# Two places of work in a four-layer graph network: row-wise endings in six later steps, and transposes held behind a maximum

## The chip, the cores and the metric

The kernel runs on one core of a Trainium2 chip. The metric is the device time of one execution in microseconds (us), the median of several runs. A core has five engines, each with its own instruction queue: PE (TensorE, matmuls), DVE (VectorE), ACT (ScalarE), POOL (GpSimd) and SP (SyncE, used here to issue DMAs). Engines wait for each other and for DMAs through semaphores.

## What is computed

A node matrix x of 4096 x 256 float32 goes through four attention layers over one adjacency matrix (4096 x 4096). Each layer adds its result to x and normalises the rows:

```python
# layer 0: additive attention, 4 heads          (the first layer)
x = _layernorm(x + _L0_gnn_ref(x, adj, L0_gnn_W, L0_gnn_a), axis=-1)
# layer 1: 4 heads of queries, keys and values  (the second layer)
x = _layernorm(x + _L1_gnn_ref(x, adj, L1_gnn_Wq, L1_gnn_bq, L1_gnn_Wk, L1_gnn_bk, L1_gnn_Wv, L1_gnn_bv), axis=-1)
# layer 2: additive attention, one head         (the third layer)
x = _layernorm(x + _L2_gnn_ref(x, adj, L2_gnn_W, L2_gnn_a), axis=-1)
# layer 3: cosine attention                     (the fourth layer)
x = _layernorm(x + _L3_gnn_ref(x, adj, L3_gnn_Wq, L3_gnn_Wk), axis=-1)
```

The two that matter here, cut to their core:

```python
def _L1_gnn_ref(x, edge, Wq, bq, Wk, bk, Wv, bv):
    q, k, v = (_split_heads(x @ W + b) for W, b in ((Wq, bq), (Wk, bk), (Wv, bv)))
    scores = jnp.einsum('hnd,hmd->hnm', q, k) / np.sqrt(HEAD_DIM)
    attn = jax.nn.softmax(scores + (edge.T - 1.0) * 10000.0, axis=-1)
    return jnp.einsum('hnm,hmd->hnd', attn, v)   # heads side by side again

def _L3_gnn_ref(features, adj, Wq, Wk):
    Qn = _cos_normalize(features @ Wq.T)
    Kn = _cos_normalize(features @ Wk.T)
    att = jax.nn.softmax(jnp.where(adj > 0, Kn @ Qn.T, NEG), axis=1)
    return 0.5 * (att @ features) + 0.5 * features   # every node has an edge to itself
```

## The kernel before

The 4096 rows are 32 tiles of 128 rows; four tiles make a block of 512 rows, so there are NB = 8 blocks of QB = 4 tiles. The rows x stay in SBUF as `X` for the whole kernel. The layers run one after the other, and each hands its last block's ending (`tail`) to the next, which weaves it into its own beginning.

How the order of instructions comes about: the program is unrolled and traced, and a planner then orders each engine's queue with a model of costs. Inside `tc.manual_schedule(engines=...)` the named engines keep the traced order. `tc.issue_after(ins)` keeps those instructions traced inside it that are on the engine of `ins` behind `ins` in that engine's queue. It adds no data dependence; the others go by the planner.

**The second layer's opening** (`multi_head_attention`, lines 727 to 825) makes keys, queries and values of all eight blocks before the attention starts. Only PE has its order written out there: `keys(0)`, the first layer's tail, `turn(1)`, and then for b from 1 to 7 `values(b - 1)` (16 matmuls of 256 columns) and `keys(b)` (32 matmuls of 512 columns; `values(6)` comes after `keys(7)`). `keys(b)` fills four PSUM banks one after the other; ACT copies each with its bias to `kT` or `qT` (L763), and DVE takes the greatest absolute value of each (`big`, L764), the queries' second half last. DVE adds the bias of the values and stores them in `V` (L781).

Every block of x is needed transposed (`xTs`). Blocks 0 and 1 are turned on PE. From block 2 on, `block_apart` (through `turning_apart`, L123 to L138) does it without PE: DVE transposes 32 x 32 squares in two halves into the tile `squares` (L129), one DMA writes them to DRAM as `far` (L133), and four DMAs read them back in their new place as `xT` (L137), all on SP's queue. `squares` has one buffer (`mh_sq`), so the next block's squares wait until the last block's write has landed. In the loop, block b + 1 is asked for in iteration b.

**The fourth layer** (`cosine_attention`) runs over blocks b of 512 queries and 32 tiles j of keys, as units (b, j). `scores` multiplies on PE (L1138), ACT takes the exponential (L1142). For two tiles at a time, a pair g = j // 2, `weights` multiplies by the mask on DVE (L1151) and `mix_weights` makes three more instructions (L443, L444, L445; the last is returned) for the seven-product scheme `product` (L453), which PE runs four units later (`LAG`). In the last block the last two pairs are without mix. The masks come from DRAM by POOL's DMA (L1070), 512 KB each, four buffers.

At the end of a block, `outputs` joins the products and `squares_far` turns them back: DVE transposes squares (L1172), SP writes four DMAs per half (`away`, L1176) and fetches the half back with one (`kept`, L1179). `outputs_far(b)` works on what was fetched (`back[b, 0]` and `back[b, 1]`): row sums (L1186), reciprocals, the rows themselves with their statistics (L1190, L156, L157), the inverse root (one DVE instruction, two of ACT, four of DVE), a scaling of each row (L186), and the store to `out` (L1203, SP). It is traced for block b - 1 when the products reach tile 10 of block b. This loop is not in a `manual_schedule`: the planner orders all engines. Only `ending`, for the last block, has its order written out.

```python
                for k in range(QB):
                    nc.vector.scalar_tensor_tensor(y[b][:, k, :], back[b, k // 2][:, k % 2, :], rden[:, k:k + 1], y[b][:, k, :],
                                                   OP.mult, OP.add)
                    one_row(mv, k, y[b][:, k, :])
                normalise([y[b][:, k, :] for k in range(QB)], mv)
                store(b, 0, QB, nc.sync)
```

Of the kernel before, what the change touches and what calls it, by code (L numbers as in the profile page):

```python
# [9 lines left out]
FP = mybir.dt.float32  # L10
# [8 lines left out]
P = 128  # L19
D = 256  # L20
# [8 lines left out]
def kernel(  # L29
# [121 lines left out]
    def block_apart(sb, once, dr, b, eng):  # L151
        return at_once(block_turning(sb, once, dr, X[:, b * QB:(b + 1) * QB, :], eng))

    def one_row(mv, k, y):
        st = fin.tile([P, 6], FP, name="bn")
        nc.vector.bn_stats(st, y)  # L156
        nc.vector.bn_aggr(mv[:, k, :], st)  # L157
# [553 lines left out]
    def multi_head_attention(w_sb, b_sb, tail, rows_of_den, rows_done, narrow_edges, ga):  # L711
# [12 lines left out]
        with ExitStack() as lay:  # L724
# [7 lines left out]
            with ExitStack() as pro:  # L732
                wp = pool(pro, "mh_w", 1)
                sb = pool(pro, "mh_in", 4)
                sq = pool(pro, "mh_sq", 1)
                own = pool(pro, "mh_o", 2)
                dr = pool(pro, "mh_far", 2, space=bass.MemoryType.DRAM)
                ps = pool(pro, "mh_ps", 6, space=PSUM)

                pv2 = pool(pro, "mh_pv", 2, space=PSUM)  # L740
                big = {n: wp.tile([P, NB, KC], FP, name=f"{n}big") for n in "qk"}
                xTs = {0: b_sb["x"]}

                def bank():
                    return ps.tile([P, QW], FP, name="g")

                def turn(b):
                    xTs[b] = transposed_block(sb, bank, b, (nc.scalar.copy, nc.scalar.copy))

                def keys(b):  # L750
                    for n, to, scale in (("k", kT, 1.0), ("q", qT, qscale)):
                        for o in range(KC):
                            pk = bank()
                            for c in range(KC):
                                nc.tensor.matmul(pk.rearrange("p (k i) -> p k i", k=QB),
                                                 w_sb[n][:, c, o * P:(o + 1) * P], xTs[b][:, c],
                                                 start=(c == 0), stop=(c == KC - 1))
                            part = to[:, o, b * QW:(b + 1) * QW]
                            if n == "q" and b > 1:

                                part, pk = (t.rearrange(how, a=QB, n=P // QB) for t, how in
                                            ((part, "p (k a n) -> p a k n"), (pk, "p (a k n) -> p a k n")))
                            nc.scalar.activation(part, pk, AF.Identity, bias=b_sb[n][:, o:o + 1], scale=scale)  # L763
                            nc.vector.tensor_reduce(big[n][:, b, o:o + 1], to[:, o, b * QW:(b + 1) * QW], AX.X, OP.max,  # L764
                                                    apply_absolute_value=True)

                def values(b):


                    for k in range(0, QB, KC):  # L770
                        pv = pv2.tile([P, KC, D], FP, name="pv")
                        for s in range(KC):
                            for c in range(KC):
                                nc.tensor.matmul(pv[:, s, :], xTs[b][:, c, k + s], w_sb["v"][:, c, :],
                                                 start=(c == 0), stop=(c == KC - 1))
                        for n in range(2):
                            j = slice(None, KC) if b > 1 else slice(None, 2 * KC - 1, 2)
                            first = 2 * b * QB + (n * QB + k if b > 1 else 2 * k + n)
                            j = slice(first, first + j.stop, j.step)
                            for r in range(2):  # L780
                                nc.vector.tensor_tensor(V[r * d:(r + 1) * d, j, :],  # L781
                                                        pv[n * d:(n + 1) * d, :, r * P:(r + 1) * P],
                                                        b_sb["v"][n * d:(n + 1) * d, r * P:(r + 1) * P].unsqueeze(1)
                                                        .to_broadcast([d, KC, P]), OP.add)

                def greatest():


                    top = {}
                    for n in "qk":  # L790
                        top[n] = wp.tile([P, KC], FP, name=f"{n}top")
                        nc.vector.tensor_reduce(top[n], big[n].rearrange("p b o -> p o b"), AX.X, OP.max)
                    nc.vector.tensor_tensor(top["q"], top["q"], top["k"], OP.mult)
                    most = wp.tile([P, KC * KC], FP, name="most")
                    for r in range(KC):
                        half = slice(r * d, (r + 1) * d)
                        pm = bank()
                        nc.tensor.matmul(pm[:, :KC], ones[half, :], top["q"][half, :], start=True, stop=True)
                        nc.vector.tensor_copy(most[:, r * KC:(r + 1) * KC], pm[:, :KC])
                    nc.vector.tensor_reduce(shift, most, AX.X, OP.max)  # L800
                    nc.vector.tensor_scalar(shift, shift, -1.0, ROOM, OP.mult, OP.add)
                    nc.vector.tensor_scalar_min(shift, shift, 0.0)

                with tc.manual_schedule(engines={mybir.EngineType.PE}):
                    keys(0)
                    tail(bank, own)
                    turn(1)
                    for b in range(1, NB):
                        if b < NB - 1:
                            xTs[b + 1] = block_apart(sb, sq, dr, b + 1, nc.sync)  # L810
                        if b < NB - 1:
                            values(b - 1)
                        keys(b)
                        if b == 2:
                            ga.spread(bank, w2_sb)
                    values(NB - 2)
                    greatest()
                    values(NB - 1)
# [293 lines left out]
    def cosine_attention(co, tail):  # L1112
# [4 lines left out]
        with ExitStack() as lay:  # L1117
# [8 lines left out]
            pa = pool(lay, "co_pa", 1, space=PSUM)  # L1126
            ps = pool(lay, "co_ps", 2, space=PSUM)
            ov = out.rearrange("(t p) d -> p t d", p=P)
            mixed, acc, prob, mix, y, back = {}, {}, {}, {}, {}, {}

            def bank():
                return ps.tile([P, QW], FP, name="g")
# [11 lines left out]
            def weights(b, g):  # L1144

                if b == 0 and g % 2 == 0:
                    t = mixed[g // 2] = keep.tile([P, 2, 4, P], FP, name=f"mixed{g // 2}")
                    mix_features(t, g // 2, nc.vector)
                    mix_sum(t, g // 2)
                z, lo = prob[b, g], 2 * g % MJ  # L1150
                nc.vector.tensor_tensor(z, z, co.mask[b, 2 * g // MJ][:, lo:lo + 2, :], OP.mult)  # L1151
                if b < NB - 1 or g < NP - LAST:
                    s = mix[b, g] = sb.tile([P, 4, HW], FP, name="mix")
                    mix_weights(s, z, nc.vector)

            def one_product(b, g, n):
                product(acc[b], prob[b, g], mix[b, g], mixed[g // 2][:, g % 2], g, n)
# [21 lines left out]
                nc.sync.dma_start(t, away.rearrange("r a m q s -> a r (m q s)"))  # L1179
                back[b, h] = t.rearrange("p (k f) -> p k f", k=2)  # L1180

            def outputs_far(b):
                mv = fin.tile([P, QB, 2], FP, name="mv")
                rden = fin.tile([P, QB], FP, name="rden4")
                for h in range(2):
                    nc.vector.tensor_reduce(rden[:, 2 * h:2 * h + 2], back[b, h], AX.X, OP.add)  # L1186
                nc.vector.tensor_scalar_mul(rden, rden, 2.0 / D)
                nc.vector.reciprocal(rden, rden)
                for k in range(QB):
                    nc.vector.scalar_tensor_tensor(y[b][:, k, :], back[b, k // 2][:, k % 2, :], rden[:, k:k + 1], y[b][:, k, :],  # L1190
                                                   OP.mult, OP.add)
                    one_row(mv, k, y[b][:, k, :])
                normalise([y[b][:, k, :] for k in range(QB)], mv)
                store(b, 0, QB, nc.sync)

            def rest(b, k, po, rden, mv):
                nc.vector.scalar_tensor_tensor(y[b][:, k, :], po, rden, y[b][:, k, :], OP.mult, OP.add)
# [88 lines left out]
                store(b, 3, 1, nc.sync)  # L1286

            units = [(b, j) for b in range(NB) for j in range(NT)]
            LAG = 4
            steps = {(0, j + n): (NB - 2 + b, step) for b, j in enumerate((1, 12)) for n, step in ((0, 3), (4, 3), (5, 1), (7, 2), (8, 3))}  # L1290
            for i in range(len(units) + LAG):
                if i < len(units):
                    b, j = units[i]
                    seen = scores(b, j)
                    if j % 2:
                        weights(b, j // 2)
                    if (b, j) == (0, 3):
                        tail(bank, cp)
                    if (b, j) == (0, 0):
# [4 lines left out]
                if i >= LAG:  # L1304
# [7 lines left out]
                    if i - LAG < len(units) - 2 * LAST:  # L1312
                        for n in range(7)[:4] if j % 2 == 0 else range(7)[4:]:
                            one_product(b, j // 2, n)
                        if j == NT - 1:
                            outputs(b)
                    if b and j == 10:
                        outputs_far(b - 1)
            with tc.manual_schedule(engines={mybir.EngineType.PE, mybir.EngineType.DVE, mybir.EngineType.Activation}):
                ending(NB - 1)  # L1320

# [89 lines left out]
```

## Time and profile before

| | |
|---|---|
| runs | 2788.82, 2796.16 and 2797.37 us, median 2796.16 us |
| profiled execution | 2794.14 us, its span 2792.4 us |
| PE busy | 2772.5 us, 99% of the span |
| DVE busy | 2290.4 us, 82% |
| ACT busy | 1702.9 us, 61% |
| POOL busy | 1082.3 us, 39% |
| second layer's opening | 723 to 813 us of the span |
| fourth layer | 2160 us to the end |

Times in a trace are counted from the start of the span. A profile names an instruction by the line of the program, so L129 or L186 may be that of a helper which several layers use; the tile's name and the time tell them apart. In the lists of waits the columns are: who waited for whom, total us, times, the longest. In the timeline they are: start, duration, engine, line, operation, written and read tiles with their shapes, how many; in square brackets stands how long the engine had been idle before, and what ended that. In the chain of waits they are start, duration and the piece of work.

### The profile page before, as it was taken

How to read it: one execution, taken by the hardware profiler on the slowest of the kernel's cores; microseconds unless marked ns; L12 is line 12 of the kernel's file. 1: busy time of each engine (PE TensorE's matmuls, PEld its weight loads, DVE VectorE, ACT ScalarE, POOL GpSimd, SP SyncE). 2: the span in 40 equal slices, each digit the busy share in tenths (PEclk: the TensorE clock that was granted, in tenths of full speed). 3: DMA queues.
4: the chain of work that ended last, by engine and by line, in shares of the span. 5: the costliest groups of instructions: out<-in, count | busy, mean ns of one | idle time of the engine just before them, and what ended most of it. 6: DMA issues, size and time to landing. Idle time of an engine off the chain costs nothing. (4 is left out here: it accounts for less than half of the span.)

```text
span 2792.4 us, 50485 instructions
## 1 busy us (share of the span) xinstructions
PE 2772.5 (99%) x19557; PEld 1449.7 (52%) x19557; DVE 2290.4 (82%) x3049; ACT 1702.9 (61%) x2668; POOL 1082.3 (39%) x1020
## 2 busy tenths in 40 slices
PE   9999999999999999999999999999999999999999
PEld 5333333333453333333333335888888777776776
DVE  8899999999677788887888878888888877776776
ACT  8899999999336666666666666465556422222222
POOL 0000100100029878778788787455455000000000
PEclk9999999999999999999999999999999999999999
DMA  7566676765339899998988988567778554444442
GB/s 207 107 142 137 138 144 130 136 143 114 69 97 193 184 178 196 192 188 184 195 182 189 190 182 187 174 199 213 181 207 238 109 82 76 77 72 78 72 74 43
DMA packets 275066, 411.94 MB, mean 148 GB/s; under 512 B 54809, under 2 KB 155657, under 8 KB 273930
## 3 DMA queue, kind: packets, MB, share of 16 engines
q0 software_dynamic: 104176, 182.74, 41.4%
q1 hardware_dynamic: 164280, 218.88, 26.2%
q10 hardware_dynamic: 6370, 7.10, 0.8%
q8 instruction: 153, 2.51, 0.4%
q14 instruction: 87, 0.71, 0.1%
HBM read 335.94 MB, written 39.40 MB: 134 GB/s over the span
## 5 line engine op out<-in xcount | busy, mean ns | idle before, releaser
L854 DVE TENSOR_TENSOR prob<-p,mask 128x1024 f32<-128x1024 f32 x512 | 619.7, 1222 | 165.9 <-ACT p L844 159.6
L844 ACT ACTIVATE p<-p,shift 128x1024 f32<-128x1024 f32 x512 | 555.7, 1088 | 319.4 <-PE p L842 319.2
L312 PE MATMUL acc<-prob,V 128*32 128x512 f32 x6144 | 664.0, 592 | 1.2 <-DVE prob L302 1.2
L299 ACT ACTIVATE prob<-row,dst 128x512 f32<-128x512 f32 x1020 | 635.1, 714 | 0.6
L302 DVE SCALAR_TENSOR_TENSOR prob<-prob,mask 128x2048 f32<-128x2048 f32 x256 | 580.4, 2286 | 25.7 <-ACT prob L299 25.0
L864 POOL TENSOR_TENSOR den<-den,prob 128x1024 f32<-128x1024 f32 x220 | 558.5, 2539 | 92.5 <-DVE prob L854 87.2
L842 PE MATMUL p<-qT,kT 64*64 64x512 f32 x4096 | 531.1, 590 | 2.2 <-DVE prob L854 2.2
L878 PE MATMUL acc<-prob,V 64*64 64x512 f32 x4096 | 529.9, 589 | 0.0
L312 PEld LDWEIGHTS acc<-prob,V 128*32 128x32 f32 x6144 | 197.3, 110 | 453.0 <-issue 432.2
L453 PE MATMUL acc<-mix,mixed 128*128 128x256 f32 x1476 | 402.1, 381 | 4.8 <-DVE mix L444 2.9
L453 PEld LDWEIGHTS acc<-mix,mixed 128*128 128x128 f32 x1476 | 278.7, 190 | 49.4 <-DVE mix L444 4.1
L878 PEld LDWEIGHTS acc<-prob,V 64*64 64x64 f32 x4096 | 157.4, 133 | 282.1 <-issue 280.3
L842 PEld LDWEIGHTS p<-qT,kT 64*64 64x64 f32 x4096 | 154.3, 133 | 279.2 <-issue 254.5
L90 POOL COPY tick<-prob 128x1 f32<-128x1 f32 x35 | 38.0, 1086 | 642.8 <-DVE prob L302 641.9
L1151 DVE TENSOR_TENSOR prob<-prob,mask 128x1024 f32<-128x1024 f32 x128 | 156.1, 1219 | 141.6 <-ACT prob L1142 141.6
L870 POOL DMA_DIRECT2D den<-prob x240 | 230.9, 962 | 61.2 <-DMA den<-prob 24.6
L1070 POOL DMA_DIRECT2D mask<-in_adjT x64 | 47.7, 745 | 532.6 <-DVE prob L1151 436.9
L453 PE MATMUL acc<-prob,X 128*128 128x256 f32 x984 | 252.6, 379 | 0.0
L453 PEld LDWEIGHTS acc<-prob,X 128*128 128x128 f32 x984 | 186.7, 190 | 78.8 <-issue 57.1
L586 DVE SCALAR_TENSOR_TENSOR prob<-r,own,mask 128x512 f32<-128x512 f32 x252 | 177.0, 743 | 49.0 <-POOL mix L445 13.0
L1142 ACT ACTIVATE prob<-p 128x512 f32<-128x512 f32 x144 | 86.0, 597 | 202.8 <-PE p L1138 202.8
L1142 ACT ACTIVATE prob<-g 128x512 f32<-128x512 f32 x112 | 66.9, 597 | 208.4 <-PE g L1138 208.4
(239 smaller groups left out, 2849.5 us busy)
## 6 DMA issues: line engine op xcount, KB each, us to landing
mask<-in_adjT SPq DMA_DIRECT2D x254, 512.0 KB
den<-prob POOLq DMA_DIRECT2D x240, 512.0 KB, 5.3
mask<-edges SPq DMA_DIRECT2D x512, 64.0 KB
mask<-in_adjT POOLq DMA_DIRECT2D x64, 512.0 KB, 5.7
edges<-in_adj POOLq DMA_DIRECT2D x32, 512.0 KB, 9.7
far<-squares SPq DMA_DIRECT2D x16, 512.0 KB
den<-prob SPq DMA_DIRECT2D x16, 512.0 KB
row<-far SPq DMA_DIRECT2D x7, 1024.0 KB
```

What stands on the lines that cost most here:

```text
L299: nc.scalar.activation(z[:, h, :], r, AF.Relu, bias=-1.0, scale=dst[:, j, h:h + 1])
L302: nc.vector.scalar_tensor_tensor(z, z, 1.0, mask[m][:, j % MJ, :].unsqueeze(1).to_broadcast([P, H, QW]), OP.add, OP.mult)
L312: nc.tensor.matmul(acc[b][h * G:(h + 1) * G, n, :], part, prob[b, j][:, h, :], start=(j == 0), stop=(j == NT - 1))
L453: nc.tensor.matmul(acc[at][:, half * HW:(half + 1) * HW], w, a, start=(g == 0 and n in (0, 2, 3, 5)), stop=(g == NP - 1), skip_group_check ...
L586: nc.vector.scalar_tensor_tensor(z[:, n, :], r, ga.own[:, j:j + 1], mask[:, n, :], OP.add, OP.mult)
L842: nc.tensor.matmul(p[c * d:(c + 1) * d, r, :], kT[half, c, at:at + d], qT[half, c, cols], start=True, stop=True)
L844: nc.scalar.activation(p, p, AF.Exp, bias=shift)
L854: nc.vector.tensor_tensor(z, p, mask[m][:, j % MJ, :].unsqueeze(1).to_broadcast([P, KC, QW]), OP.mult)
L864: nc.gpsimd.tensor_tensor(to, to, flat, OP.add)
L870: nc.gpsimd.dma_start(to, flat, accum_op=OP.add)
L878: nc.tensor.matmul(acc[b][c][r * d:(r + 1) * d, :], V[half, j, r * d:(r + 1) * d], prob[b, j][half, r, :], start=(j == 0), stop=(j == NH - 1))
L1151: nc.vector.tensor_tensor(z, z, co.mask[b, 2 * g // MJ][:, lo:lo + 2, :], OP.mult)
```

## The change

In the fourth layer `outputs_far(b)` is cut into six steps. `weights` now returns the last mix instruction, and the loop keeps it as `mixes`. Steps 0 to 5 for block b - 1 are traced when the products have reached tiles 15, 17, 19, 21, 23 and 25 of block b, after the scores and weights of the unit four further on; each is inside `issue_after(mixes)`, so that its DVE instructions stay behind that mix. Step 0 makes the sums and reciprocals, steps 1 and 2 two rows each, step 3 begins the root, step 4 ends it and scales two rows, step 5 scales two and stores.

In the second layer `keys` returns its last maximum, and `block_apart(b + 1)` is traced inside `issue_after` of the maximum that `keys(b - 1)` returned. The first call of the loop (block 2) has none; block 3 is held behind block 1's, and so on to block 7 behind block 5's. Only the DVE squares are held by it, as the DMAs are issued from SP.

```diff
                             nc.scalar.activation(part, pk, AF.Identity, bias=b_sb[n][:, o:o + 1], scale=scale)
-                            nc.vector.tensor_reduce(big[n][:, b, o:o + 1], to[:, o, b * QW:(b + 1) * QW], AX.X, OP.max,
-                                                    apply_absolute_value=True)
+                            last = nc.vector.tensor_reduce(big[n][:, b, o:o + 1], to[:, o, b * QW:(b + 1) * QW], AX.X,
+                                                           OP.max, apply_absolute_value=True)
+                    return last
...
                     turn(1)
+                    last = None
                     for b in range(1, NB):
                         if b < NB - 1:
-                            xTs[b + 1] = block_apart(sb, sq, dr, b + 1, nc.sync)
+                            with tc.issue_after(getattr(last, "ins", last)) if last is not None else nullcontext():
+                                xTs[b + 1] = block_apart(sb, sq, dr, b + 1, nc.sync)
                         if b < NB - 1:
                             values(b - 1)
-                        keys(b)
+                        last = keys(b)
...
                 if b < NB - 1 or g < NP - LAST:
                     s = mix[b, g] = sb.tile([P, 4, HW], FP, name="mix")
-                    mix_weights(s, z, nc.vector)
+                    return mix_weights(s, z, nc.vector)
...
-            def outputs_far(b):
...
+            def outputs_far(b, step, seen):
+
+                with tc.issue_after(getattr(seen, "ins", seen)):
+                    if step == 0:
+                        rden = fin.tile([P, QB], FP, name="rden4")
+                        for h in range(2):
+                            nc.vector.tensor_reduce(rden[:, 2 * h:2 * h + 2], back[b, h], AX.X, OP.add)
+                        nc.vector.tensor_scalar_mul(rden, rden, 2.0 / D)
+                        nc.vector.reciprocal(rden, rden)
+                        norm[b] = rden, fin.tile([P, QB, 2], FP, name="mv")
+                    elif step < 3:
+                        rden, mv = norm[b]
+                        for k in (2 * step - 2, 2 * step - 1):
+                            nc.vector.scalar_tensor_tensor(y[b][:, k, :], back[b, k // 2][:, k % 2, :], rden[:, k:k + 1],
+                                                           y[b][:, k, :], OP.mult, OP.add)
+                            one_row(mv, k, y[b][:, k, :])
+                    elif step == 3:
+                        norm[b] += begin_root(norm[b][1])
+                    else:
+                        _, mv, v, r, n = norm[b]
+                        if step == 4:
+                            end_root(v, r, n)
+                        for k in (2 * step - 8, 2 * step - 7):
+                            scale_row(y[b][:, k, :], mv, r, k)
+                        if step == 5:
+                            store(b, 0, QB, nc.sync)
...
-            LAG = 4
+            LAG, mixes = 4, None
...
                     if j % 2:
-                        weights(b, j // 2)
+                        mixes = weights(b, j // 2) or mixes
...
-                    if b and j == 10:
-                        outputs_far(b - 1)
+                    if b and j in (15, 17, 19, 21, 23, 25):
+                        outputs_far(b - 1, (j - 15) // 2, mixes)
```

More of the change, by code (lines that the diff above doesn't have):

```diff
@@ L1128, in cosine_attention @@
             ov = out.rearrange("(t p) d -> p t d", p=P)
-            mixed, acc, prob, mix, y, back = {}, {}, {}, {}, {}, {}
+            mixed, acc, prob, mix, y, back, norm = {}, {}, {}, {}, {}, {}, {}
             def bank():
@@ L1180, in squares_far @@
                 back[b, h] = t.rearrange("p (k f) -> p k f", k=2)
-            def outputs_far(b):
[L1183 to L1194, printed above, removed]
+            def outputs_far(b, step, seen):
[23 more added lines that the diff above has]
+                            store(b, 0, QB, nc.sync)
             def rest(b, k, po, rden, mv):
```

## Prediction

> **What bounds the kernel now.** I read the page first. TensorE (PE) is busy 99% of 2792.4 us; its clock is full in nearly all slices. So only time in which PE stands still, or runs slowly after a pause, can be won. Next, PE's waits by stretch. In the fourth layer (2160 to 2793 us) there is one wait of PE itself, and one group of VectorE (DVE) waits that could be behind it:
>
> ```profile
> DVE rden L1186 <- DMA kept<-away: 16.8, 8, 6.9
> ...
> PE acc L453 <- DVE mix L444: 2.9, 1, 2.9
> ```
>
> [...]L1186 is the first instruction of `outputs_far`: it reads the rows fetched back from DRAM. The timeline shows how one wait becomes the other:
>
> ```profile
> 2573.62 0.74 POOL L1070 DMA_DIRECT2D mask<-in_adjT  x1 [8.73 <-DVE prob L1151]
> ...
> 2573.64 0.56 SPq L1179 DMA_DIRECT2D kept<-away  x1
> ...
> 2581.00 0.69 DVE L1186 TENSOR_REDUCE rden<-kept 128x2 f32<-128x512 f32 x1 [6.95 <-DMA kept<-away]
> 2581.60 0.42 DVE L444 TENSOR_TENSOR mix<-prob,mix 128x256 f32<-128x256 f32 x1
> ...
> 2582.07 1.27 PE L453 MATMUL acc<-mix,mixed 128*128 128x256 f32 x4 [2.88 <-DVE mix L444]
> ...
> 2583.14 1.91 PE L1138 MATMUL g<-T,T 128*128 128x512 f32 x2
> ```
>
> The fetch is issued in the same moment as a 512 KB mask load and takes 7.4 us. The planner has put L1186 between L443 and L444, so two instructions of the running pair of tiles stand behind it. PE then waits 2.88 us and runs slowly (1.91 us for a score that takes 1.02 elsewhere). The chain of waits has the same place:
>
> ```profile
> 2557.72 5.54 DMA away<-kept
> 2564.59 8.97 DMA away<-kept
> 2573.64 7.34 DMA kept<-away
> ```
>
> What does it cost? The first `away` issues of the seven blocks start at 2251.52, 2327.99, 2403.91, 2479.82, 2555.73, 2636.48 and 2712.39: distances 76.47, 75.91, 75.92, 75.91, 80.75, 75.91. The undisturbed block is 75.91 us, so the fifth event costs 4.84 us, the first (DVE waited 4.05 us) 0.56, the others nothing though DVE waited up to 1.78. Together 5.40 us.
>
> The second layer's opening (723 to 813 us) has three DVE waits for the squares buffer, 11.3 us, the longest 6.1:
>
> ```profile
> 733.02 1.30 DVE L129 STREAM_TRANSPOSE squares<-X 128x512 f32<-128x512 f32 x2 [6.09 <-DMA far<-squares]
> 734.25 0.64 DVE L764 TENSOR_REDUCE kbig<-kT 128x1 f32<-128x512 f32 x1
> ...
> 736.86 0.42 ACT L230 ACTIVATE neg<-neg 128x256 f32<-128x256 f32 x1 [5.16 <-DVE neg L229]
> ...
> 737.18 1.05 ACT L119 COPY xT<-g 128x512 f32<-128x512 f32 x2
> ...
> 737.80 3.70 PE L755 MATMUL g<-xT,wk_sb 128*128 128x512 f32 x8 [1.19 <-ACT xT L119]
> ```
>
> Read upwards: PE waits for ScalarE's (ACT) copies of block 1, these stand behind a `neg` that waits for DVE, and DVE stands still with block 3's squares, as the single buffer still holds block 2's. Everything behind is late too. Undisturbed, `keys` takes 6.87 us and `values` 3.44 (760.77 to 767.64, 767.64 to 771.09). Here `keys(1)` starts at 737.80 rather than 736.44 (1.36), lasts 7.27 (0.40), and `values(1)` lasts 4.08 (0.64): 2.40 us lost.
>
> **The Trainium skill.** "Perfetto Trace Analysis", Tensor Engine Instruction, says that ACT and DVE are strict FIFO: a blocked instruction blocks all behind it. Both pictures agree. "DMA: Bandwidth & Descriptors", Queues, rings and completion order, says that each engine shares itself in turn among the queues with work, so a mask load slows a fetch beside it; the trace agrees in that fetch (7.4 us, against 5.5 at 2268.42). "TensorE: Matmul & The Clock Gate", Part 1, says that an idle stretch halves the array's clock for a while; the 1.91 us after the pause, against 1.02, fits.
>
> **The change, part by part. (a) Fourth layer.** Instructions, bytes and engines stay the same; `outputs_far` becomes six steps, each held behind the last mix instruction (L445) of the running pair. Step 0 is traced after unit (b, 19), pair 9; the fetch starts after pair 1. A pair takes 4.74 us: eight pairs are 37.9 us, so step 0 starts about 38 us after the first `away` issue. The latest landing seen is 25.3 us after it (2581.0 - 2555.7), so 13 us remain and DVE should not wait. What stands behind each step on DVE is the next pair's mask product. DVE's pair is 1.22 + 0.69 + 0.42 + 0.42 = 2.75 us and then about 1.87 idle (L1151 waits for ACT). Step 0: 2 x 0.683 + 0.164 + 0.172 = 1.70. Steps 1 and 2: 2 x (0.467 + 0.418 + 0.174) = 2.12 each. Step 3: 0.17 plus two ACT instructions of 0.2. Step 4: 4 x 0.16 and two scalings of 0.35, 1.3. Step 5: 0.7. Only steps 1 and 2 exceed the idle, by 0.25 us each. PE reads a pair's mix about 4.06 us after it is ready (2769.54 against 2773.60), so 0.5 us is hidden; without that cover it would cost 0.5 us a block, 3.5 in all. Step 3's exponentials stand in ACT's queue before later `prob`; in the third event, ACT waited 1.71 us for this and PE lost nothing.
>
> The store (SP) moves to about 61 us after the first `away`, before the next at 75.9: nothing of SP's is behind it then. For the last block it is issued near 2770 rather than 2742.69, while the final stores start at 2787.68; 512 KB should be gone by then. Step 5 is behind pair 13's mix at 2769.54, where DVE is free until 2771.41: free. Buffers: the fetched rows are needed until step 2, at pair 11, and overwritten after the next block's end; `y` has two buffers and its next user comes later than the store. Sum of (a): -5.40 us.
>
> **(b) Second layer.** Block 3's squares now stand behind the last queries' maximum of block 1 (750.53), and so on. The 6.09 us wait at 727 goes: DVE does the maxima and the row tail about 4 us earlier, `neg` and the copies are ready near 734.5, before PE needs them at 736.4. That returns the 1.36 us and most of the 1.04 behind it. Bounds: 0 to 2.40, I take 2.0. The price is lateness. From the end of block 7's squares (780.14) its turned rows are landed by 786.5: 6.4 us through two DMAs in SP's queue. After `keys(5)` ends (788.28) the maximum ends at 789.89, two halves of squares take 1.30 and the trip 6.4: 797.6, against `keys(7)` at 798.60, which has no `values` before it. 1.0 us remain. Blocks 3 to 6 have 3.44 us more. DVE's values sums (L781) come 1.3 us later, and PE takes that buffer again only 17 us later. Before SP's next issues (817.76) the queue is empty. Sum of (b): -2.0.
>
> **Sum.** Profiled execution 2794.14 - 5.4 - 2.0 = 2786.7 us. The runs shown are 2788.82, 2796.16 and 2797.37. 2794.14 - 5.40 = 2788.74 is almost the lowest: I read the scatter as more or fewer such fetch waits, an inference. So I do not add the 2.0 us by which the median lies above the profiled execution; against the median it is -9.5 us, or -0.34%. About 0.3% (8.4 us) is what a measurement can tell from no change.
>
> **Rivals. B: the opening returns nothing.** The order on DVE is the planner's there, and another instruction may hold the copies, or the 1.0 us of block 7 is used up. For: the whole tail of the first layer sits on DVE there. Against: DVE stands idle 6 us just before. 2794.14 - 5.4 = 2788.7.
>
> **C: the steps press on the pairs.** DVE's idle is smaller than steps 1 and 2, and ACT may wait at step 3 as at 2281.55 (3.95 us, where that pair of PE took 0.30 longer). At 0.3 to 0.6 us a block over seven: 2.1 to 4.2 back, hence 2789 to 2791. Against: in four events all of this work within two or three pairs cost nothing.
>
> **D: slower, the turn becomes the second layer's bound.** If the planner puts the eight L781 (3.5 us) ahead of the squares and the write takes 7.5 us, as block 2's did (725.53 to 733.02), rather than 2.7, the maximum's 1.6, 3.5, 1.3 and the trip of 11.2 make 17.6 against the 13.75 from the end of `keys(b-1)` to the start of `keys(b+1)`: 3.9 us late at block 3, again at block 5, and 7.3 at block 7, where only 10.3 lie between: 15.1 in all, so 2794.14 - 5.4 + 15.1 = 2803.8. It costs from a trip of 7.3 us behind those sums, and outweighs the fourth layer's gain from 8.0. Against: the mask loads that slowed that write are over by then (DMA is idle from 744 on).
>
> The change not doing what it says: were the planner's order unchanged by the edges, the time would be 2794; but the squares before 750 us and L1186 before pair 9 are ruled out by them.
>
> **How the numbers follow.** Forecast A 0.62, B 0.18, C 0.12, D 0.08. A spans 2784.5 to 2788; with B and C the range is 2784.5 to 2791, leaving out D and a little. Faster by over 0.3% (below 2787.8): most of A and a little of B, 0.58; within 0.3%: 0.34; slower: 0.08.
>
> **What would show it.** Right: no DVE wait for `kept<-away`; `away` distances of 75.9 in all blocks; no PE wait in front of `keys(1)`; squares of block 3 after the maximum of block 1. Wrong: PE waiting in front of `keys(7)` or `keys(3)`, ACT waiting over 4 us for step 3's variances (L182), or a run-to-run scatter as wide as before, which would mean that it came from elsewhere.

## The result and the profile after

| | before | after |
|---|---|---|
| median | 2790.87 us (2788.21 to 2797.37, 14 runs) | 2786.06 us (2785.25 to 2788.96, 14 runs) |
| profiled execution | 2794.14 us, span 2792.4 | 2785.99 us, span 2784.2 |
| PE busy | 2772.5 us | 2768.9 us |

The ratio after to before is 0.9982, 95% interval [0.9975, 0.9988]: about 5 us less. The forecast of 2786.7 us lies 0.6 us above the median of the changed kernel. The gain is smaller than forecast: 0.18% rather than 0.34%, since before's median over 14 runs is 2790.87 us and not the 2796.16 of the three runs that I had. The interval lies clear of 1, so the prediction's 0.3% as the least that can be told from no change was too coarse.

In the program after the change `outputs_far`'s sums are L1191 (L1186 before), the mask product L1154 (L1151), the away writes L1179 and the fetch L1182 (L1176, L1179), the mask load L1073 (L1070). The first view is the timeline of the fifth block after, with the same moment as the one shown of before:

```profile
2568.89 0.56 SPq L1182 DMA_DIRECT2D kept<-away  x1
2570.28 0.74 POOL L1073 DMA_DIRECT2D mask<-in_adjT  x1 [8.73 <-DVE prob L1154]
...
2590.16 0.43 DVE L445 TENSOR_TENSOR mix<-prob,mix 128x256 f32<-128x256 f32 x1
2590.50 1.27 DVE L1191 TENSOR_REDUCE rden<-kept 128x2 f32<-128x512 f32 x2
...
2595.24 0.87 DVE L1198 SCALAR_TENSOR_TENSOR y<-kept,rden,y 128x256 f32<-128x256 f32 x2
...
2596.69 0.30 DVE L157 BATCH_NORM_AGGREGATE mv<-bn 128x2 f32<-128x6 f32 x2
2597.19 1.23 DVE L1154 TENSOR_TENSOR prob<-prob,mask 128x1024 f32<-128x1024 f32 x1 [0.20 <-ACT prob L1145]
```

The sums come straight behind L445, with no bracket: DVE did not wait. They start 38.1 us after the block's first `away` issue (2552.38); the fetch had been issued 21.6 us earlier. After step 1 DVE is still idle for 0.20 us before the next mask product, waiting for ACT, so the step fits. In the list of waits of this layer the two rows shown of before (`rden` for `kept<-away`, `acc` for `mix`) no longer occur. The seven first `away` issues start at 2248.73, 2324.64, 2400.55, 2476.46, 2552.38, 2628.29 and 2704.20: six distances of 75.91 or 75.92.

The second view is the timeline of the second layer's opening after:

```profile
732.63 0.42 ACT L230 ACTIVATE neg<-neg 128x256 f32<-128x256 f32 x1 [1.11 <-DVE neg L229]
...
732.96 1.05 ACT L119 COPY xT<-g 128x512 f32<-128x512 f32 x2
...
736.27 3.60 PE L755 MATMUL g<-xT,wk_sb 128*128 128x512 f32 x8
...
746.31 0.67 DVE L764 TENSOR_REDUCE qbig<-qT 128x1 f32<-128x512 f32 x1
...
746.91 1.29 DVE L129 STREAM_TRANSPOSE squares<-X 128x512 f32<-128x512 f32 x2
```

ACT's copies of block 1 end at about 734.0, over 2 us before PE needs them, and `keys(1)` starts with no wait. Block 3's squares stand behind the last maximum of block 1, as the edge says. DVE's three waits for the squares buffer (11.3 us before) are gone.

To see where a difference lies I cut each execution at four instants: the start of `keys(0)`, the first attention score of the second layer, the first and the last of the fourth layer's first `away` issues. "Opening" is between the first two, "middle" between the second and third, "blocks lose" is the sum of six distances less 6 x 75.91. The end after the last issue is 80.0 us in all of them. The experiments are told below. Each row is one profiled execution, in us, and experiments ran on different chips:

| execution | opening | middle | blocks lose | its time |
|---|---|---|---|---|
| before | 89.59 | 1438.49 | 5.40 | 2794.14 |
| before, second profile (e12_plain) | 89.79 | 1441.93 | 4.85 | 2797.22 |
| before, third profile (e13_plain) | 89.71 | 1440.67 | 1.77 | 2793.85 |
| after | 87.22 | 1438.25 | 0 | 2785.99 |
| after again (e9_both) | 87.21 | 1438.65 | 0 | 2786.61 |
| opening alone (e1_opening) | 87.21 | 1438.61 | 0.68 | 2786.88 |
| opening alone again (e10_opening) | 87.21 | 1440.58 | 1.95 | 2790.95 |
| fourth layer alone (e2_fourth) | 89.25 | 1438.48 | 0 | 2787.53 |
| fourth layer alone again (e11_fourth) | 89.41 | 1437.30 | 0 | 2787.56 |
| late, in one piece (e4_onepiece) | 89.77 | 1439.87 | 0 | 2790.20 |
| six steps, early (e5_early) | 89.50 | 1440.26 | 9.8 | 2799.41 |
| two squares buffers (e3_twobuf) | 91.87 | 1441.42 | 6.5 | 2800.45 |
| only block 3 held (e8_block3) | 87.21 | 1443.96 | 1.7 | 2793.56 |
| one block back (e6_oneback) | 133.92 | 1443.96 | 1.0 | 2839.41 |

From before to after, profile against profile, the span falls by 8.2 us: 2.37 in the opening, 5.40 in the blocks, 0.24 in the middle, 0.18 ahead of `keys(0)`.

### The profile page after: what moved, and what is told of

It reads as the page before. It is cut to its first block, busy times and chain, and to the rows that moved or that the text cites. A ratio compares the mean times of both kernels' runs of the same rounds, so it can differ in the third digit from the quotient of the medians.

```text
span 2784.2 us, 50486 instructions
## 1 busy us (share of the span) xinstructions
PE 2768.9 (99%) x19557; PEld 1449.1 (52%) x19557; DVE 2299.5 (83%) x3049; ACT 1703.4 (61%) x2668; POOL 1080.8 (39%) x1020
## 5 line engine op out<-in xcount | busy, mean ns | idle before, releaser
L1154 DVE TENSOR_TENSOR prob<-prob,mask 128x1024 f32<-128x1024 f32 x128 | 156.3, 1221 | 142.9 <-ACT prob L1145 142.9
L1073 POOL DMA_DIRECT2D mask<-in_adjT x64 | 47.6, 743 | 526.9 <-DVE prob L1154 508.3
```

## The experiments

The first four shared one chip and the kernel before on it (median 2791.68 us, 2787.37 to 2797.84, 56 runs). Those runs form two heaps, 38 from 2787.4 to 2792.7 and 18 from 2794.0 to 2797.8.

**The opening alone.** The kernel before with the second layer's part of the change only.

```diff
-                            xTs[b + 1] = block_apart(sb, sq, dr, b + 1, nc.sync)
+                            with tc.issue_after(getattr(last, "ins", last)) if last is not None else nullcontext():
+                                xTs[b + 1] = block_apart(sb, sq, dr, b + 1, nc.sync)
...
-                        keys(b)
+                        last = keys(b)
```

> The second layer's part alone, the fourth layer as before. My theory: the opening falls from 89.6 us (723.4 to 813.0) to 87.2 us as in the kernel after, without a PE wait in front of keys(1), and the fourth layer keeps its waits for the fetched rows, some 10 to 20 us of DVE waits in total and blocks of 75.9 us plus now and then 0.5 to 5 us. Time: 2.4 us below before, in every run alike; the runs stay scattered over 5 us or more. Rival (the scatter comes from the opening, where a far write lies beside loads): the scatter shrinks to about 2 us here and the time falls by 4 us or more.

Measured: 2787.79 us (2786.03 to 2788.73, 12 runs), ratio 0.9985 [0.9976, 0.9993]. In the profile the opening takes 87.21 us, the whole 2.4 less. The fourth layer still waits for its fetches, as its list of waits says (total, times, longest):

```profile
DVE rden L1189 <- DMA kept<-away: 10.4, 6, 4.0
...
PE acc L453 <- DVE mix L444: 0.2, 1, 0.2
```

The longest wait here is 4.0 us where before had 6.9, though this layer's instructions stand in the same order on every engine: the same program part can lose 0.68 us in one execution and 5.40 in another. The gain by the median (3.9 us) is more than the opening's 2.4 and the scatter of 2.7 us less than I expected: both figures are nearer to the rival's than to mine. The interval holds 2.4 and 3.9 alike. The repetition below comes back to it.

**The fourth layer alone.** The six late steps, the opening as before.

```diff
-                    if b and j == 10:
-                        outputs_far(b - 1)
+                    if b and j in (15, 17, 19, 21, 23, 25):
+                        outputs_far(b - 1, (j - 15) // 2, mixes)
```

> The fourth layer's part alone, the second layer as before. My theory: no DVE wait for the fetched rows, all seven distances of the first away issues at 75.9 us, opening still 89.6 us; median 2 to 3 us below that of before (5.4 below a run with waits such as the profiled one), and the runs within about 2 to 3 us of each other. Rival (scatter from the opening): scatter as wide as before.

Measured: 2788.46 us (2786.32 to 2792.11, 21 runs), ratio 0.9984 [0.9978, 0.9991]. All six distances are 75.91 or 75.92 and DVE does not wait for `kept<-away`. But the runs still scatter over 5.8 us: what goes up and down from run to run is not the fetch waits alone.

**Late, but in one piece.** Are the steps needed, or only the later place? `outputs_far` is left whole and traced at tile 15, behind the mix of pair 9.

```diff
-                    if b and j == 10:
-                        outputs_far(b - 1)
+                    if b and j == 15:
+                        with tc.issue_after(getattr(mixes, "ins", mixes)):
+                            outputs_far(b - 1)
```

> The fourth layer's part alone, as late as in the kernel after but in one piece: all of it behind the mix of pair 9. If lateness is what counts (my theory): no DVE wait for the fetched rows. Two reductions, two small ones and four rows (5.9 us) then stand ahead of the next pair's mask product where DVE has 1.9 us idle, so that mask is about 4 us late, as much as the 4.06 us that PE has in hand: 0 to 0.5 us of PE per block, 0 to 3.5 us in all; time equal to the part alone in six steps, or up to 3.5 us more. If splitting is what counts (rival): blocks of 77 us or more, nothing gained over before.

Measured: 2788.71 us (2786.04 to 2791.28, 21 runs), ratio 0.9986 [0.9979, 0.9993], blocks 75.91 or 75.92 throughout. The place does it; no loss shows from doing it in one piece.

**A second squares buffer.** If the opening's loss came from the single buffer, a second one should win it without any edge.

```diff
-                sq = pool(pro, "mh_sq", 1)
+                sq = pool(pro, "mh_sq", 2)
```

> Before with two buffers of squares in the second layer's opening instead of the later squares; fourth layer as before. If the single buffer were the cause (rival), the 6 us DVE wait would go and the opening take 87.2 us, time 2.4 us below before. My theory is that the order is the cause: DVE's order now has block 3's squares and then block 4's in front of the maxima of block 0, and block 4's wait for block 2's write just as block 3's did; so a wait of about 6 us and a PE wait of 1 to 3 us in front of keys(1) stay, opening 89 to 92 us, time 0 to 3 us above before.

Measured: 2794.57 us (2792.29 to 2800.45, 13 runs), ratio 1.0011 [1.0002, 1.0019]: slower by 2.9 us by the medians. The timeline of its opening shows why:

```profile
724.72 1.89 DVE L129 STREAM_TRANSPOSE squares<-X 128x512 f32<-128x512 f32 x3
726.53 0.65 DVE L764 TENSOR_REDUCE kbig<-kT 128x1 f32<-128x512 f32 x1
...
733.26 1.30 DVE L129 STREAM_TRANSPOSE squares<-X 128x512 f32<-128x512 f32 x2 [6.08 <-DMA far<-squares]
...
735.05 1.29 DVE L129 STREAM_TRANSPOSE squares<-X 128x512 f32<-128x512 f32 x2
...
738.60 1.05 ACT L119 COPY xT<-g 128x512 f32<-128x512 f32 x2
...
739.22 3.33 PE L755 MATMUL g<-xT,wk_sb 128*128 128x512 f32 x4 [2.69 <-ACT xT L119]
```

The planner puts a further block's squares into the place that became free. The same 6.1 us wait stands at the same place in DVE's queue, now with more squares around it, the copies come at 738.6 and PE waits 2.69 us instead of 1.19. The opening takes 91.87 us, 2.3 more than before. So it is the order on DVE that costs, not the buffer as such: with the second buffer the planner only takes the next stall.

**Six steps, but early.** The reverse: the six steps are traced at tiles 5 to 15, behind the mixes from pair 4 on. This one and the next two ran on another chip (before there: 2795.88 us, 2790.65 to 2804.62, 33 runs).

```diff
-                    if b and j == 10:
-                        outputs_far(b - 1)
+                    if b and j in (5, 7, 9, 11, 13, 15):
+                        outputs_far(b - 1, (j - 5) // 2, mixes)
```

> The fourth layer's six steps, each behind a mix, but from pair 4 on instead of pair 9 (products at tile 5 instead of 15); second layer as before. If lateness is what counts (my theory): DVE waits for the fetched rows again, about as in the kernel before (several waits of 1 to 4 us, the fifth block's of 4 to 8 us when its fetch meets a mask load), blocks 1 and 5 longer than 75.91 us by 0.5 to 6 us, time as before or up to 3 us less. If cutting it up is what counts (rival): all blocks 75.91 us and the time of the late six steps, 2788.5 us.

Measured: 2796.27 us (2793.55 to 2806.48, 13 runs), ratio 1.0005 [0.9995, 1.0015]. Its waits in the fourth layer:

```profile
DVE rden L1188 <- DMA kept<-away: 24.6, 7, 9.1
...
PE acc L453 <- DVE mix L444: 6.6, 2, 5.0
```

Cut into steps but early, the waits are back, in this profile longer than in before's first (24.6 us against 16.8), and the gain is gone. Together with the run in one piece this settles it: lateness gives the fourth layer's gain, not the cutting.

**Only block 3 held.** Of the edges to blocks 3 to 7, the first alone.

```diff
+                            with tc.issue_after(getattr(last, "ins", last)) if b == 2 else nullcontext():
+                                xTs[b + 1] = block_apart(sb, sq, dr, b + 1, nc.sync)
```

> The second layer's part alone, and of it only block 3 held behind block 1's maximum; blocks 4 to 7 as before, fourth layer as before. My theory: only the first of the three DVE waits cost PE anything, so the opening takes 87.2 us here too and the time equals that with all five held, 2787.8 us. Rival: the later waits (1.6 and 3.6 us in before) or their order matter as well, opening 88 us or more.

Measured: 2791.70 us (2789.17 to 2794.14, 21 runs), ratio 0.9982 [0.9975, 0.9988]; opening 87.21 us. The first edge does all of it; the four others change nothing that shows.

**Squares one block back.** How near is the turn to becoming the bound (my slower rival)? From block 3 on the squares stand behind the maximum of the block just before, instead of two back.

```diff
-                        keys(b)
+                        last = keys(b)
+                        if 1 < b < NB - 1:
+                            with tc.issue_after(getattr(last, "ins", last)):
+                                xTs[b + 1] = block_apart(sb, sq, dr, b + 1, nc.sync)
```

> The second layer's part alone, but each block's squares held behind the maximum one block back instead of two; fourth layer as before. The sum of the prediction says: from the end of keys(b) the maximum takes 1.6 us, the squares 1.3, the trip through DRAM 6.4: 9.3 us, where values(b) gives 3.44 us of cover for blocks 3 to 6 and nothing for block 7. PE late by 5.9 us four times and by 9.3 us once, 33 us, and more if PE's clock falls after each pause (up to 10 us more): opening 120 to 130 us, time 2821 to 2831 us. Rival (the trip is shorter or hidden in another way): opening under 100 us.

Measured: 2838.07 us (2835.24 to 2839.41, 4 runs), ratio 1.0150 [1.0136, 1.0164]. The list of waits of its opening has one new row:

```profile
PE g L755 <- DMA xT<-far: 34.1, 5, 9.8
```

And the timeline of the last of the five:

```profile
831.05 0.69 DVE L764 TENSOR_REDUCE qbig<-qT 128x1 f32<-128x512 f32 x1 [1.03 <-ACT qT L763]
831.65 1.29 DVE L129 STREAM_TRANSPOSE squares<-X 128x512 f32<-128x512 f32 x2
832.97 0.34 SPq L133 DMA_DIRECT2D far<-squares  x1
...
835.67 1.73 SPq L137 DMA_DIRECT2D xT<-far  x4
840.13 6.21 PE L755 MATMUL g<-xT,wk_sb 128*128 128x512 f32 x8 [9.85 <-DMA xT<-far]
```

PE stands still for 9.85 us, against the 9.3 from the end of `keys` that the prediction added up (1.6, 1.3 and 6.4). The difference is the trip: from the end of the squares (832.94) to the start of `keys` it is 7.2 us, not 6.4. The five waits sum to 34.1 us; the same sum gives 4 x 5.9 + 9.3 = 32.9. The opening is longer still, 133.9 us and not 120 to 130: after each pause the first half of `keys` (8 of the 16 matmuls that a profile shows of it) takes 5.3, 6.3, 6.7, 5.2 and 6.2 us instead of 3.60, together 11.8 us more. So a turn that comes too late does stop PE, at about the price that was added up, and the change stays clear of it by going two blocks back. The rival's own case, sums of the values ahead of the squares and a slow write, was not run.

**Do the parts add?** On a further chip (before: 2791.23 us, 2787.63 to 2798.01, 41 runs) the changed kernel and its two parts ran side by side, with the edits shown above.

> The changed kernel once more, beside its two parts on one chip. In the traces the parts add exactly (opening -2.4, fourth layer -5.4). Theory that both gains are real and constant: ratio about 0.9972 (-7.8 us). Theory that the kernel before only sometimes pays the fetch waits in full, so that the traces of single executions overstate the gain: ratio about 0.998 (-5 us).

> The opening alone once more: second layer's blocks held, fourth layer as before. By the trace -2.4 us, ratio 0.9991. In an earlier measurement it gave 0.9985, over 12 runs within 2.7 us and without the upper clump that the kernel before has. If the opening removes that clump, the runs are again within 3 us and the ratio 0.9985; if that was chance, runs from the upper clump appear, scatter is 5 us or more, and the ratio is 0.9990 or above.

> The fourth layer alone once more, opening as before. By the trace -5.4 us, ratio 0.9981; an earlier measurement gave 0.9984 with a scatter of 5.8 us. If the two parts add, this ratio's loss and that of the opening alone sum to that of both within 0.0006.

Measured: both 2786.61 us (2783.31 to 2788.06, 21 runs), ratio 0.9980 [0.9973, 0.9986]; the opening alone 2787.80 (2785.46 to 2790.95, 13 runs), 0.9989 [0.9981, 0.9997]; the fourth layer alone 2788.81 (2787.56 to 2791.80, 13 runs), 0.9993 [0.9985, 1.0001]. The parts give 0.0011 + 0.0007 = 0.0018 against 0.0020: they add. But 0.0020 is 5.6 us and not 7.8; the interval ends just short of 0.9972. The fourth layer's part is the one that falls short: by the ratios 2 and 4.5 us in the two measurements, not 5.40, and this one's interval takes in no change. For the opening alone the expectation decides nothing: the ratio is between its two cases and the scatter is 5.5 us, yet none of its 25 runs in both measurements is above 2791, where 26 of before's 97 are above 2793.5. The fourth layer alone has none above 2792.2 in 34: in these runs either part by itself removes before's upper heap.

**Two more profiles of the kernel before.** They come from one more chip, one run each. In all kernels with the early reading the mask load of the fifth block starts 17.9 us after the first `away` issue; the second fetch starts when the away writes have landed, 16.7 to 18.0 us after it. I took it for a race that is won or lost. The kernel is unchanged.

> The kernel before, unchanged, for a second profile of it. Theory of the race: in the fifth block the mask load starts 17.9 us after the first away issue whatever happens, and the second fetch starts when its away writes have landed, now just before, now just after it. In an execution at 2788 to 2792.5 us the fetch starts 0.4 to 1.5 us ahead of the mask load, takes about 5.5 us, DVE's wait is at most 4.5 us and the fifth block loses at most 1.2 us (77.1 us or less). In one at 2794 us or more the fetch starts after the mask load, takes 7.3 us or more and the block loses 4.8 us or more. Rival: the time has nothing to do with it, the fifth block is 80.75 us as in the first profile and the difference lies in the middle, from the first score of the second layer to the first away issue.

> As the plain one before it: a third profile of the kernel before. Theory of the race: fifth block 77.1 us or less where the second fetch starts ahead of the mask load, 80 us or more where it starts behind it, and the execution's time on the side that goes with it (up to 2792.5, or 2794 and more). Rival: 80.75 us again whatever the time.

The third profile (2793.85 us), timeline of the fifth block:

```profile
2576.44 0.56 SPq L1179 DMA_DIRECT2D kept<-away  x1
...
2577.60 0.74 POOL L1070 DMA_DIRECT2D mask<-in_adjT  x1 [8.73 <-DVE prob L1151]
...
2582.09 0.69 DVE L1186 TENSOR_REDUCE rden<-kept 128x2 f32<-128x512 f32 x1 [4.05 <-DMA kept<-away]
2582.69 0.42 DVE L444 TENSOR_TENSOR mix<-prob,mix 128x256 f32<-128x256 f32 x1
...
2583.16 1.13 PE L453 MATMUL acc<-mix,mixed 128*128 128x256 f32 x4
```

The second profile (2797.22 us), the same place:

```profile
2578.99 0.56 SPq L1179 DMA_DIRECT2D kept<-away  x1
2579.16 0.74 POOL L1070 DMA_DIRECT2D mask<-in_adjT  x1 [8.73 <-DVE prob L1151]
...
2585.48 0.69 DVE L1186 TENSOR_REDUCE rden<-kept 128x2 f32<-128x512 f32 x1 [5.89 <-DMA kept<-away]
2586.08 0.41 DVE L444 TENSOR_TENSOR mix<-prob,mix 128x256 f32<-128x256 f32 x1
...
2586.55 1.13 PE L453 MATMUL acc<-mix,mixed 128*128 128x256 f32 x4 [1.82 <-DVE mix L444]
```

Read the first two lines of each: the fetch is 1.16 us ahead of the mask load in one, 0.17 in the other, and 0.02 behind it in the first profile of before. From fetch to reading it takes 5.65, 6.49 and 7.36 us, and the fifth block loses 0.56, 2.39 and 4.84. So the same kernel does pay this differently from execution to execution, and the rival (80.75 us whatever the time) is wrong. But my theory was too simple. It is not just won or lost: the second profile is ahead of the mask load and still loses 2.39 us (its fourth block loses 1.63 more, after a DVE wait of 5.12, with a fetch 1.24 us ahead of a mask load). And the meeting is the smaller part of the wait. In the six blocks of these three profiles where DVE waits 0.7 us or less for it, the second fetch is issued 12.5 to 13.7 us after the first `away` issue; in the fifth it is issued 16.7 to 17.9 us after it, and even the third profile's fetch of 5.65 us leaves a DVE wait of 4.05. The writes land that much later there; why, no run shows. And it does not go with the time as I wrote: 2793.85 lies between the two bands of the expectation, and 2797.22 is high mostly because the middle took 3.4 us longer than in the first profile, in stages that nobody touched.

## Why the prediction was right, and where it was not

- **The time.** 2786.7 us was predicted, 2786.06 measured. The sum was made from one profiled execution, and profile against profile it is good: -7.4 predicted, -8.15 found (2794.14 to 2785.99). That it meets the median so closely is in part luck. The profile used has a middle of 1438.49 us, like the 1438.25 after; from the two later profiles of before, on another chip and with middles of 1441.93 and 1440.67, the same sum (the blocks' loss and 2.0) gives 2790.4 and 2790.1.
- **The gain, and the chances.** This is where it failed. I gave 0.58 to a gain of over 0.3% and 0.34 to one within it; it is 0.18%, and the interval ends at 0.25%. The step that failed is the one after the sum: "2794.14 - 5.40 = 2788.74 is almost the lowest: I read the scatter as more or fewer such fetch waits, an inference", by which a single execution's 5.40 us became the worth of the change, beside a median of three runs. Before's median is 2790.87 us over 14 runs, 3.3 below the profiled execution. The fetch waits do vary (5.40, 4.85 and 1.77 us in three profiles), and the one used has the most to give. The inference about the scatter was half right: with both parts the runs spread over 3.7 and 4.8 us in two measurements, against 9.2 and 10.4 of before beside them. But with the fetch waits alone gone they still spread over 4.2 and 5.8; in the table the middle alone goes from 1437.3 to 1440.6 on the chip of e9 to e11.
- **(a) Fourth layer: mechanism right, size right for that execution, too large for the median.** Step 0 comes 38.1 us after the first `away` issue (38 predicted), no wait is left, all distances are 75.91 or 75.92. Of 5.40 us, the two measurements of this part alone show 2.0 and 4.5 by their ratios. The overrun of 0.25 us in steps 1 and 2 did not occur: step 1 lasts from 2595.24 to 2596.99, 1.75 us, where single durations added up to 2.12; neighbouring instructions overlap in the records.
- **(b) The opening: mechanism right, term mis-sized.** I took 2.0 of the possible 2.40; it is 2.37 between the profiles and nearly the same in all kernels with the edge. Holding back 0.4 us of what lies behind the first 1.36 was too careful. It needs only the first of the five edges.
- **The rivals.** B (the opening returns nothing, 2788.7) did not happen: 87.2 us in five profiles. C (steps press on the pairs) did not: with the late reading no block is longer than 75.92, and ACT's longest wait for step 3 (L182) is 0.9 us. D (the turn becomes the bound) did not; the kernel one block back confirms the mechanism. One sum of D is off: it costs from a trip of 7.3 us at blocks 3 and 5, but at block 7, where 10.3 us less the 6.4 of work remain, from 3.9.
- **Right for a reason I had not seen.** The prediction had one fetch that happened to collide with a mask load. The runs show that the mask load's place, 17.9 us behind the first `away` issue, is the same in every profile, and that this fetch, late already, sits within 1.2 us of it in each profile of before. The late reading wins by being indifferent to it: the fetch may take 5 or 9 us, and may start 12 or 18 us after that issue.
- **Open:** why the opening alone gave no run above 2791 in 25, although its fourth layer reads early, as before's does. The mean clock recorded with each run gives a hint: 17 of before's 130 runs in the experiments have 0.998 or 0.997, all of them at 2794.9 us or more, and none of the 136 of the changed kernel, of either part, in one piece or with only block 3 held has less than 0.999. The profiles with 0.998 and 0.997 (two buffers, early steps) hold 6.8 and 10.2 us at half clock before their end, the first of before 3.4. So part of the upper heap probably had PE at half clock for longer than any profile of before shows; where, is not known. Open too is what moves the middle by 2 to 3 us. PE's own listed waits from 860 to 2240 us, mostly for DVE in the second and third layers, sum to 4.6, 6.4 and 6.0 us in the three profiles of before: that is 1.8 of the second's 3.4 us more, and 1.4 of the third's 2.2.

## What to carry to other kernels

A reading that stands close behind its fetch is a wait waiting to happen on an engine that works in order: put it late, behind work that doesn't need it, and ask for no more than that (cutting it up gave nothing here, and in the opening a second buffer even cost time). Before a gain read from one profile is called the worth of a change, take two or three profiles of the kernel before: the loss from one and the same wait was 5.40, 4.85 and 1.77 us here. When a step is delayed, add up its trip against the next use; here that sum came to 9.3 us for the last block where 9.85 were measured.

## What the runs showed of the hardware

**What a pause of PE costs depends on where it falls.** A DVE wait for the fetch becomes an idle PE about 4.06 us shorter: 5.12 to 1.06, 5.89 to 1.82, 6.95 to 2.88. The block's loss is the idle time plus 0.57 us for the first two (1.63 and 2.39), but 4.84 for 2.88 us idle, plus 1.96. With 1.82 us idle the next score takes the usual 1.02 us, with 2.88 it takes 1.91. In the kernel one block back, pauses of 5.0 to 9.9 us cost 1.6 to 3.1 us each afterwards. But the length alone does not decide. The next view gives, for PE in single stretches of the span, their length, PE's busy time (matmuls), the granted clock, the DMA engines' busy share and their GB/s. The first two lines are the kernel before with its pause of 2.88 us, the others the kernel with only block 3 held, where PE waits 3.68 us (1738.05 to 1741.73) for a DVE instruction of the second layer's end:

```profile
2579.52:2582.93 3.41, 0.85 (x4) 1.00 0.14 30
2582.93:2586.35 3.42, 3.42 (x8) 0.50 0.00 0
...
1736.59:1740.00 3.41, 1.46 (x11) 1.00 0.00 0
1740.00:1743.41 3.41, 1.68 (x10) 1.00 0.59 195
1743.41:1746.83 3.42, 3.42 (x18) 1.00 1.04 367
```

The shorter pause halved the clock, the longer did not. In each of the fourteen traces all changes of the clock lie whole multiples of 3.41 us apart, and the half-speed stretches before the end last 3.41, 6.83 or 10.24 us. Cut each trace into these windows of 3.41 us, from 60 us on to the clock's last change near the end: of those at full clock, all eleven in which the trace shows PE idle for 2.01 us or more are followed by half clock, and none with 1.95 us or less is. The 3.68 us fell into two windows, 1.95 and 1.73 us idle. A pause of 2.10 us with early steps (1739.04 to 1741.13), nearly all in one window, was enough. So the same pause can cost one execution more than another. The Trainium skill, "TensorE: Matmul & The Clock Gate", Part 1, puts the fall of the clock at an idle window of some 3.4 us; the length of the window agrees here, but it need not be idle throughout, and the measurement decides.

**A fetch issued together with a mask load is slow.** From the issue of the fifth block's second fetch to its reading it took 6.49 us when issued 0.17 us ahead of the mask load, 7.36 at 0.02 behind, and 8.3 and 8.7 at 0.08 and 0.09 behind in the kernels with two buffers and with early steps. Issued 1.16 us ahead it took 5.65, which is no more than elsewhere: in the three profiles of before, the second fetches for which DVE waited and that were issued 0.4 us or more ahead took 4.8 to 5.7 us, but for one. That one, in the second profile's fourth block, took 6.79 at 1.24 ahead, and no run shows why. That transfers of two queues share the engines in turn, as "DMA: Bandwidth & Descriptors", Queues, rings and completion order, says, fits the meeting. That the mask load is the cause is read from the times: no kernel here moved it.
